# A two-layer relational graph network on one core: which engine copies turned rows, sums and row numbers, and how two queues share the copying of single rows

## The chip, the cores and the metric

The kernel runs on one core of one Trainium2 chip. The core has five engines that work side by side, each in the order of its own instructions: TensorE (PE in the profile; PEld are its weight loads), VectorE (DVE), ScalarE (ACT), GpSimd (POOL) and SyncE (SP). ACT, SP and POOL also issue DMAs, each on a queue of its own (ACTq, SPq, POOLq in the profile). The metric is the device time of one run in microseconds (us); for the kernel before, the median of three runs is 23771.16 us.

## The reference

Two relational graph layers over the same 800,000 edges and 50,000 nodes of 128 features, then a residual and a layer norm; cut to what matters:

```python
def _rgcn_layer(h, src, dst, rel, basis, w_comp, loop_w, bias):
    W = jnp.einsum('rb,bio->rio', w_comp, basis)          # 16 relations from 8 bases
    seg = dst.astype(jnp.int32) * N_REL + rel.astype(jnp.int32)
    agg = jax.ops.segment_sum(h[src], seg, num_segments=N_ENT * N_REL)
    agg = agg.reshape(N_ENT, N_REL, -1)
    msg = jnp.einsum('nri,rio->no', agg, W)
    return jax.nn.relu(msg + h @ loop_w + bias)

h = _rgcn_layer(x, src, dst, rel, basis1, w_comp1, loop_w1, bias1)
h = _rgcn_layer(h, src, dst, rel, basis2, w_comp2, loop_w2, bias2)
out = _layernorm(x + h)
```

The kernel is given 850,000 edges sorted by `dst`, among them one loop (src = dst) for each node. It takes the loops out and treats them apart as "own" rows.

## The kernel before

**Tiles, half chunks, chunks.** In each layer the 800,000 remaining edges are cut into 6250 tiles of 128 edges. Five tiles (`PER`) are a half chunk, ten a chunk; there are 1250 half chunks and 625 chunks (`C`). For each tile the 128 source rows, 512 bytes each, are brought from memory (from `x` in the first layer, from `H1`, named `H` in the profile, in the second) into a buffer `g`, and TensorE multiplies them with `hot`, a 128 x 96 matrix that VectorE has made from the edges' weights and targets (8 bases times a window of 12 nodes; line 1145). The products of a half chunk stand in one bank `pa` and are copied to `aT` (line 1101: by ACT in the first and last eight chunks, by DVE in between, `COPIED`). For four chunks at a time `aT` is multiplied with the bases (line 816), the sum is copied out (`by_slot`, line 821, ACT), turned (line 826), spread to nodes by DVE (`slots`, line 799) and added up per group of 512 nodes (`pn`, line 861). Beside this runs the work on own rows: a group's 512 rows are turned by TensorE (line 746), copied out (`hT`, line 752, ACT), multiplied with the bases (line 766), weighted and summed by DVE (lines 773 and 781).

**How rows come.** Most tiles are gathered by GpSimd: one indirect DMA per tile (line 187), whose 128 row numbers stand in a column of `at`. `at` holds numbers for 20 tiles and is made from the 16-bit list `src` by a cast on ACT (line 1075), three buffers in turn. The ring of `g` has 30 buffers, so a gather waits for the product that read its buffer 30 tiles before. The fifth tile of some half chunks is not gathered: `takers` gives every ninth half chunk to SP and, shifted by four, every ninth to ACT (`SPANS = (9, 9)`). `row_by_row` copies its 128 rows one at a time: a load of 32 row addresses from `far` into registers (line 1041), then 32 DMAs of 512 bytes, each with its address from a register (line 1048), four times. Each of the two queues has three buffers for this (`HELD`). In the program a copy is written in between the other work, a few rows after each product, over the nine half chunks before half chunk q - 8 (`LEAD`).

**Order.** All engines run under an order written out by hand: what the Python loop issues first stands first on its engine. So an ACT copy stands behind the row DMAs that were issued before it, and the row DMAs behind it wait while it waits.

**The beginning.** The edge list is turned into `src`, `far` and the other lists in pieces of rows (`ROWS`: half chunks 0 to 15, 16 to 119, and so on). In the first layer a step of `later_rows` is taken per chunk, and a piece is forced to be done at chunk c when 2 * (c + FETCH + earliest) goes beyond it, with `earliest` = 10.

Of the kernel before, what the change touches and what calls it, by code (L numbers as in the profile page):

```python
# [55 lines left out]
S = K * WN  # L56
# [4 lines left out]
LK = 64  # L61
LBITS = 10
FETCH = 2
WIDE = 20
AT = 8
PER = 5
Q = AT // 2
# [1 line left out]
WEIGHTS = AT * PER * 8  # L69
BITS_AT_ONCE = BANK - WEIGHTS  # L70
RING = 6
SPANS = (9, 9)
LEAD = 8
THEN = 3
COPIED = 8
# [6 lines left out]
BATCH = 4  # L82
# [11 lines left out]
def tile_rgcn_resnorm(  # L94
# [15 lines left out]
    nc = tc.nc  # L110
# [4 lines left out]
    C = -(-M // (K * P))  # L115
# [91 lines left out]
    src = consts.tile([P, 2 * C * HALF], U16, name="src")  # L207
# [4 lines left out]
    ]  # L212
    came = [[tc.alloc_semaphore(f"came{i}_{j}") for j in range(SEMS)] for i in range(len(APART))]
    uses = [0] * len(APART)
    earliest = (max(SPANS) + LEAD + 1) // 2 + 1
    far = consts.tile([P, len(ROWS), P], I32, name="far")

    def takers():

        of, first = {}, max(SPANS) + LEAD + 6  # L220
        for i, span in enumerate(SPANS):
            for q in range(first + span * i // len(SPANS), 2 * C - LEAD, span):
                while q in of:
                    q += 1
                of[q] = i
        return of

    taken_by = takers()
# [383 lines left out]
    def chunked():  # L612
        with (
# [5 lines left out]
            def ks(c):  # L619
                return min(K, -(-M // P) - c * K)  # L620

            ALONE, halves_of = C - BATCH - 1, [None]

            def nodes(g):
                return min(GN, N - g * GN) // J
# [21 lines left out]
            def told_apart(of, by, width, c, name):  # L647

                k = sum(ks(i) for i in range(c, min(c + Q, C)))
                apart = hp.tile([P, Q * K, width], U8, name=name, bufs=1)[:, :k]  # L650
                nc.vector.tensor_tensor(
                    apart,
                    of[:, None, :width].to_broadcast([P, k, width]),
                    by[:, c * K : c * K + k, None].to_broadcast([P, k, width]),
                    op=OP.is_equal,
                )
                return apart
# [70 lines left out]
            def from_itself(g, of, n):  # L728

                m = nodes(g)  # L730
                at, rows_in = g % T * (P // T), m // A
                if g == 0:
                    load_own(0, T, of)
                h = owns[at : at + rows_in]
                if g % T == 0:
                    for some in loop_weights(g, n):
                        if some is not None:
                            lws[:] = [some]
                        yield
                else:  # L740
                    yield
                lw = lws[0]
                po = ps_o.tile([P, BANK], F32, name="po")
                few = P // A
                for i in range(A * J):
                    nc.tensor.transpose(  # L746
                        po[:, i * few : i * few + rows_in], h[:, i, :], ident[at : at + rows_in, at : at + rows_in]
                    )
                    if i % (2 * A) == 2 * A - 1:
                        yield  # L750
                hT = sb.tile([P, J, P], F32, name="hT", bufs=2)
                nc.scalar.copy(  # L752
                    hT.rearrange("d j (p a) -> d a j p", a=A)[:, :, :, :rows_in],
                    po.rearrange("d (a j p) -> d a j p", a=A, j=J)[:, :, :, :rows_in],
                )
                hTs[g] = hT
                yield
                ls = sb.tile([P, J, D], F32, name="ls")
                lss[g] = ls
                few = BANK // D  # L760
                if g == 0:
                    nc.vector.tensor_copy(by[:, NB, :], BIAS[n])
                for j in range(J):
                    for b in range(0, NB, few):
                        hb = ps_o.tile([P, BANK], F32, name="po")
                        nc.tensor.matmul(  # L766
                            hb[:m],
                            hT[:, j, :m],
                            BASIS[n][:, b : b + few, :].rearrange("p b d -> p (b d)"),
                            start=True,  # L770
                            stop=True,
                        )
# [8 lines left out]
                    nc.vector.tensor_reduce(ls[:m, j, :], by[:m].rearrange("p b d -> p d b"), AX.X, OP.add)  # L781
                    yield
# [27 lines left out]
            def slots_of_batch(c, aT, st, n):  # L810

                for _ in range(2):
                    yield
                ps = ps_o.tile([P, BANK], F32, name="po")
                for b in range(NB):
                    nc.tensor.matmul(  # L816
                        ps[:, : BATCH * S], BASIS[n][:, b, :], aT[:, b, :], start=b == 0, stop=b == NB - 1
                    )
                yield
                by_slot = sb.tile([P, BATCH * S], F32, name="by_slot", bufs=1)  # L820
                nc.scalar.copy(by_slot, ps[:, : BATCH * S])
# [56 lines left out]
            def finish(g, n):  # L878

                m = nodes(g)  # L880
                ls = lss.pop(g)[:m]
                total = sums.pop(g)[:m].rearrange("p (j d) -> p j d", j=J)
                nc.vector.tensor_tensor(total if n else ls, total, ls, op=OP.add)
                if n == 0:
                    yield
                    nc.scalar.activation(ls, ls, AF.Relu)
                    for _ in range(THEN):
                        yield
                    nc.sync.dma_start(of_group(H1, g), ls)
                else:  # L890
                    nc.vector.scalar_tensor_tensor(ls, total, 0.0, xws.pop(g)[:m], op0=OP.max, op1=OP.add)
                    yield
                    yield from normed(ls, J, m, ls, sb)
                    for _ in range(THEN):
                        yield
                    nc.sync.dma_start(of_group(out, g), ls)  # L896
                yield

            def done(steps):
                for _ in steps:  # L900
# [39 lines left out]
            for n, of in enumerate((x, H1)):  # L940
# [82 lines left out]
                def row_by_row(i):  # L1023
# [1 line left out]
                    by, kind = APART[i]  # L1025
                    flat = bass.AP(tensor=of.tensor, offset=of.offset, ap=[[1, N * D]]).bitcast(U8)
                    mine = sorted(q for q in taken_by if taken_by[q] == i)
                    for q, before in zip(mine, [mine[0] - SPANS[i], *mine]):
                        while now[1] < before - LEAD:
                            yield  # L1030
                        steps = PER * (q - before)
# [23 lines left out]
                        held[q * PER + PER - 1] = to, sem, 16 * P * (use // SEMS + 1), group  # L1055
                        assert now[1] < q

                def place_in_ring(t):
# [10 lines left out]
                def numbers(b):  # L1069

                    m = min(WIDE, tiles - b * WIDE)
                    if m <= 0:
                        return
                    at = hp.tile([P, WIDE], I32, name="at", bufs=3)[:, :m]
                    made = nc.scalar.copy(at, src[:, b * WIDE : b * WIDE + m])  # L1075
# [21 lines left out]

                def taken_out():

                    by_vector = COPIED <= now[0] < C - COPIED  # L1100
                    (nc.vector.tensor_copy if by_vector else nc.scalar.copy)(*to_take)  # L1101

                numbered, held = {}, {}
                numbers(0)
                now, made = [0, 0], [0]
                owning = own_of_all()
                copying = [row_by_row(i) for i in range(len(APART))]
                for c in range(C):
                    now[0] = c
                    if n == 0 and c:  # L1110

                        next(coming, None)
                        while ready[0] + 1 < len(ROWS) and 2 * min(C, c + FETCH + earliest) > ROWS[ready[0] + 1]:
                            next(coming)
                    if c == 0:
                        fetch(range(RING * PER))
# [261 lines left out]
```

## Time and profile before

| | |
|---|---|
| median of 3 runs | 23771.16 us (23735.37 to 23829.01) |
| the profiled execution | 23546.47 us, of it 23544.3 us span |
| PE busy | 11586.5 us (49%) |
| DVE busy | 11688.0 us (50%) |
| ACT busy (copies and activations, without issuing DMAs) | 838.5 us (4%) |
| POOL busy | 11364.1 us (48%) |
| gathers by POOL | 5979 in each layer |
| rows copied one at a time by SP, by ACT | 17408 and 17280 in each layer |

Issuing DMAs is not counted as busy: how full the queues of SP and ACT are is seen in the timeline, where a row such as "SPq L1048 DMA_DIRECT2D g<-in_x_dram x64" is a stretch in which 64 single rows were issued (register loads between them are inside the stretch). In groups, "| a, b | c <-X d" reads: busy for a us in total, mean b ns of one, c us of idle time of the engine just before, of which X ended d.

### The profile page before, as it was taken

The page shows a single profiled execution, that of the slowest core. Times are in us where ns is not written, and L with a number is a line of the kernel's source. Part 1 is how long each engine was busy: PE and PEld are TensorE (multiplying, and loading weights), DVE is VectorE, ACT ScalarE, POOL GpSimd, SP SyncE. Part 2 cuts the span into 40 slices and gives each one's busy share as a digit, 9 for nine tenths or more (in the row PEclk, how much of TensorE's full clock was granted, in tenths as well). Part 3 has the DMA queues.
Part 4 walks back from the last instruction along what each step waited for, and adds up shares of the span by engine and source line. Part 5 has one row for each costly group of instructions (what it writes and reads, how often), then busy time and mean ns, then how long its engine had stood idle before and what let it go on. Part 6 is the DMA issues. An engine that isn't in the chain of part 4 may idle for free. (4 is left out here: it accounts for less than half of the span.)

```text
span 23544.3 us, 262043 instructions
## 1 busy us (share of the span) xinstructions
PE 11586.5 (49%) x43954; PEld 7419.2 (32%) x43954; DVE 11688.0 (50%) x14173; ACT 838.5 (4%) x1873; POOL 11364.1 (48%) x11991
## 2 busy tenths in 40 slices
PE   4544445444554544444554444444544444444445
PEld 3333333333333333233333333332332333333233
DVE  5555555555544444444544444444444444444445
ACT  0000000000000000000000000000000000000000
POOL 5544445444544444444454444444444444444444
PEclk7776677776677676676767776776766777766767
DMA  2111111111111111111111111111111111111111
GB/s 58 50 47 43 46 46 49 48 44 44 47 44 40 40 39 40 39 39 39 42 45 43 42 42 42 42 42 41 42 42 42 43 42 41 42 41 42 42 42 41
DMA packets 591750, 1014.42 MB, mean 43 GB/s; under 512 B 270531, under 2 KB 342979, under 8 KB 583794
## 3 DMA queue, kind: packets, MB, share of 16 engines
q0 software_dynamic: 384528, 791.33, 13.3%
q1 hardware_dynamic: 133308, 186.60, 2.5%
q10 hardware_dynamic: 72208, 19.62, 0.4%
q14 instruction: 1353, 11.08, 0.2%
q8 instruction: 353, 5.78, 0.1%
HBM read 924.87 MB, written 71.59 MB: 42 GB/s over the span
## 5 line engine op out<-in xcount | busy, mean ns | idle before, releaser
L187 POOL DMA_INDIRECT g<-H,at x5979 | 5658.7, 946 | 6136.5 <-PE pa L1145 3621.1
L187 POOL DMA_INDIRECT g<-in_x_dram,at x5979 | 5680.7, 950 | 5939.1 <-PE pa L1145 3438.7
L1145 PE MATMUL pa<-hot,g 128*128 128x96 f32 x25000 | 4289.6, 317 | 5679.3 <-DMA g<-H 2934.2
L1145 PEld LDWEIGHTS pa<-hot,g 128*128 128x128 f32 x25000 | 4239.8, 236 | 7638.2 <-DMA g<-H 3007.6
L773 DVE TENSOR_TENSOR by<-po,lw 128x512 f32<-128x512 f32 x1568 | 1074.7, 686 | 6412.4 <-PE po L766 4721.4
L861 PE MATMUL pn<-slots,own 120*128 120x512 f32 x4128 | 2738.5, 789 | 2075.2 <-issue 1117.4
L816 PE MATMUL po<-aT,basis 128*128 128x480 f32 x4960 | 2572.1, 681 | 1366.1 <-DVE aT L1101 752.6
L766 PE MATMUL po<-basis,hT 128*128 128x512 f32 x3136 | 2118.3, 764 | 1753.8 <-ACT hT L752 924.0
L1101 DVE COPY aT<-pa 128x480 f32<-128x480 f32 x2436 | 1567.6, 648 | 2672.5 <-PE pa L1145 2143.6
L816 PEld LDWEIGHTS po<-aT,basis 128*128 128x128 f32 x4960 | 1122.5, 233 | 2626.5 <-issue 2478.6
L781 DVE TENSOR_REDUCE ls<-by 128x128 f32<-128x1152 f32 (+1 forms) x784 | 1653.6, 2109 | 549.1 <-DMA out_dram<-ls 444.1
L668 DVE TENSOR_REDUCE fixed<-terms 128x80 f32<-128x1280 f32 x1250 | 1864.6, 1492 | 30.3
L639 DVE TENSOR_TENSOR terms<-kinds,fixed 128x1280 f32<-128x1280 uint8 x1250 | 1848.2, 1479 | 10.9
L861 PEld LDWEIGHTS pn<-slots,own 120*128 120x128 f32 x4128 | 884.8, 243 | 2749.4 <-issue 1753.9
L952 DVE TENSOR_TENSOR hot<-fixed,own 128x960 f32<-128x960 f32 x1250 | 1438.7, 1151 | 21.3 <-remote 3.0
L766 PEld LDWEIGHTS po<-basis,hT 128*128 128x128 f32 x3136 | 595.2, 236 | 1803.4 <-ACT hT L752 936.8
L799 DVE TENSOR_TENSOR slots<-po,which 120x1024 f32<-120x1024 f32 (+1 forms) x630 | 760.9, 1208 | 441.4 <-remote 304.8
L826 PE MATMUL po<-ident,by_slot 128*120 128x128 f32 x1240 | 311.5, 343 | 743.5 <-DVE by L773 423.0
L1075 ACT CAST at<-src 128x20 int32<-128x20 uint16 x626 | 129.5, 207 | 12082.0 <-issue 8490.2
L826 PEld LDWEIGHTS po<-ident,by_slot 128*120 128x120 f32 x1240 | 190.9, 188 | 764.1 <-issue 634.0
L840 DVE TENSOR_SCALAR own<-col,node 120x256 f32<-120x256 f32 (+1 forms) x1250 | 423.2, 339 | 8.6 <-PE pn L861 7.9
L746 PE MATMUL po<-ident,h_own 32*128 32x32 f32 x3136 | 328.2, 249 | 60.1 <-issue 54.1
(144 smaller groups left out, 3556.2 us busy)
## 6 DMA issues: line engine op xcount, KB each, us to landing
g<-in_x_dram SPq DMA_DIRECT2D x17408, 0.5 KB
g<-H SPq DMA_DIRECT2D x17408, 0.5 KB
g<-in_x_dram ACTq DMA_DIRECT2D x17280, 0.5 KB
g<-H ACTq DMA_DIRECT2D x17280, 0.5 KB
g<-in_x_dram,at POOLq DMA_INDIRECT x5979
g<-H,at POOLq DMA_INDIRECT x5979
H<-ls SPq DMA_DIRECT2D x97, 256.0 KB
xw<-in_x_dram SPq DMA_DIRECT2D x97, 256.0 KB
```

Of the source, the lines that this page charges most:

```text
L187: return nc.gpsimd.indirect_dma_start(out=to, out_offset=None, in_=of, in_offset=bass.IndirectOffsetOnAxis(ap=idx, axis=0))
L639: nc.vector.tensor_tensor(terms, kinds[:, :, None, :].to_broadcast([P, k, NB, NR]), table[:, None, :, :].to_broadcast([P, k, NB, NR]), op= ...
L668: nc.vector.tensor_reduce(to[:, : ks(i)], terms, AX.X, OP.add)
L766: nc.tensor.matmul(hb[:m], hT[:, j, :m], BASIS[n][:, b : b + few, :].rearrange("p b d -> p (b d)"), start=True, stop=True,)
L773: nc.vector.tensor_tensor(by[:m, b : b + few, :], hb[:m].rearrange("p (b d) -> p b d", d=D), lw[:m, j, g % T, b : b + few, None].to_broadc ...
L781: nc.vector.tensor_reduce(ls[:m, j, :], by[:m].rearrange("p b d -> p d b"), AX.X, OP.add)
L799: nc.vector.tensor_tensor(to[:k], of[:k, :, None, :].to_broadcast([k, pair, J, D]), which[:k, c : c + pair, :, None].to_broadcast([k, pair ...
L816: nc.tensor.matmul(ps[:, : BATCH * S], BASIS[n][:, b, :], aT[:, b, :], start=b == 0, stop=b == NB - 1)
L861: nc.tensor.matmul(sums[g], own, of[:k].rearrange("s j d -> s (j d)"), start=c == first(g), stop=c == final(g),)
L952: nc.vector.tensor_tensor(hot[:, : ks(c)], pm[:, : ks(c), :, None].to_broadcast([P, ks(c), NB, WN]), own[:, : ks(c), None, :].to_broadcast ...
L1101: (nc.vector.tensor_copy if by_vector else nc.scalar.copy)(*to_take)
L1145: product = nc.tensor.matmul(pa[:, i * NB * WN : (i + 1) * NB * WN], row, hot[:, k + i].rearrange("e b w -> e (b w)"), start=True, stop=Tr ...
```

## The change

VectorE makes three kinds of copies that ScalarE made: `hT`, `by_slot` and `at`, except in the first and last eight chunks of a layer. The spans become 9.25 half chunks for SP and 8.75 for ACT. And at the beginning the second piece of rows is forced in chunk 3, where it was forced in chunk 1 (`SOONEST` = 4 in the place of `earliest` = 10, which keeps its value). The assertions are not part of the program that runs.

```diff
+SOONEST = 4
-SPANS = (9, 9)
+SPANS = (9.25, 8.75)
...
-    earliest = (max(SPANS) + LEAD + 1) // 2 + 1
+    earliest = (round(max(SPANS)) + 1 + LEAD + 1) // 2 + 1
...
-        of, first = {}, max(SPANS) + LEAD + 6
+        of, first = {}, round(max(SPANS)) + LEAD + 6
         for i, span in enumerate(SPANS):
-            for q in range(first + span * i // len(SPANS), 2 * C - LEAD, span):
+            at = first + span * i / len(SPANS)
+            while at < 2 * C - LEAD:
+                q = int(at)
                 while q in of:
                     q += 1
                 of[q] = i
+                at += span
...
-                nc.scalar.copy(
+                copy_by()(
                     hT.rearrange("d j (p a) -> d a j p", a=A)[:, :, :, :rows_in],
...
-                nc.scalar.copy(by_slot, ps[:, : BATCH * S])
+                copy_by()(by_slot, ps[:, : BATCH * S])
...
+            def copy_by():
+
+                return nc.vector.tensor_copy if COPIED <= now[0] < C - COPIED else nc.scalar.copy
...
-                    for q, before in zip(mine, [mine[0] - SPANS[i], *mine]):
+                    for q, before in zip(mine, [mine[0] - round(SPANS[i]), *mine]):
...
-                    made = nc.scalar.copy(at, src[:, b * WIDE : b * WIDE + m])
+                    made = copy_by()(at, src[:, b * WIDE : b * WIDE + m])
...
-                        while ready[0] + 1 < len(ROWS) and 2 * min(C, c + FETCH + earliest) > ROWS[ready[0] + 1]:
+                        soon = FETCH + (earliest if ready[0] else SOONEST)
+                        while ready[0] + 1 < len(ROWS) and 2 * min(C, c + soon) > ROWS[ready[0] + 1]:
                             next(coming)
```

What moves on the engines. On ACT's queue in the first layer, around one Relu of a finished group (the same group in both); "1x512 x17" are 17 single rows in a row, `far` the load of 32 addresses. Before:

```order
L1048 DMA g_122<-in_x_dram 1x512 x9
L886 ACTIVATE ls<-ls 128x512
L1048 DMA g_122<-in_x_dram 1x512 x3
L1075 CAST at<-src 128x20
L1048 DMA g_122<-in_x_dram 1x512 x17
L821 COPY by_slot<-po 128x480
L1048 DMA g_122<-in_x_dram 1x512 x3
L1041 TENSOR_LOAD far
L1048 DMA g_122<-in_x_dram 1x512 x32
```

And of the change:

```order
L1057 DMA g_121<-in_x_dram 1x512 x2
L891 ACTIVATE ls<-ls 128x512
L1057 DMA g_121<-in_x_dram 1x512 x30
L1050 TENSOR_LOAD far
L1057 DMA g_121<-in_x_dram 1x512 x32
L1050 TENSOR_LOAD far
L1057 DMA g_122<-in_x_dram 1x512 x32
```

The casts and copies that stood between the rows are gone; between two Relus ACT now issues rows and nothing else. Over the whole program SP issues 33792 rows and 1056 loads (before 34816 and 1088), ACT 35584 and 1112 (before 34560 and 1080); POOL gathers 11958 tiles in both.

On DVE at the same group, of the change; `ls<-pn,ls` is the group's last sum, `aT` the copy of a half chunk's products, `by` and `ls` the work on own rows:

```order
L673 TENSOR_REDUCE fixed<-terms 128x80
L757 COPY hT<-po 128x4x128
L888 TENSOR_TENSOR ls<-pn,ls 128x512
L961 TENSOR_TENSOR hot<-fixed,own 128x960
L845 TENSOR_SCALAR own<-col_128,node_126 120x128
L1114 COPY aT<-pa 128x5x8x12
L1089 CAST at<-src 128x20
L778 TENSOR_TENSOR by<-po,lw 128x512
L1114 COPY aT<-pa 128x5x8x12
L643 TENSOR_TENSOR terms<-kinds,fixed 128x1280
```

Without `hT` and `at` this is the order of before. Of `at`, `by_slot` and `hT`, 610, 306 and 192 stand on DVE now, and 16, 4 and 4 on ACT (before 626, 310 and 196 on ACT).

At the beginning, on TensorE, before (`both` is the first product that makes the second piece of rows, g_95 the buffer of the tenth tile):

```order
L1145 MATMUL pa<-hot,g_94 128x96
L1145 MATMUL pa<-hot,g_95 128x96
L483 MATMUL pa<-ident,both 128x104 x5
L483 MATMUL pa<-ident,l_word 128x104 x5
L483 MATMUL pa<-ident,relf 128x104 x5
```

And of the change (g_115 is the buffer of the thirtieth tile, `h_own` are own rows):

```order
L1159 MATMUL pa<-hot,g_114 128x96
L1159 MATMUL pa<-hot,g_115 128x96
L751 MATMUL po<-ident,h_own 128x32 x8
L487 MATMUL pa<-ident,both 128x104 x5
L487 MATMUL pa<-ident,l_word 128x104 x5
L487 MATMUL pa<-ident,relf 128x104 x5
```

The second piece stood behind ten tiles and stands behind thirty. In SP's order the loads for the first own rows (`lrel`, `h_own`) now stand ahead of the loads of the second run of edges (`d_i` and three more), where they stood behind them; the first row copy stands behind all of these in both.

More of the change, by code (lines that the diff above doesn't have):

```diff
@@ L620, in ks @@
                 return min(K, -(-M // P) - c * K)
-            ALONE, halves_of = C - BATCH - 1, [None]
+            ALONE, halves_of, now = C - BATCH - 1, [None], [0, 0]
             def nodes(g):
@@ L649, in told_apart @@
                 k = sum(ks(i) for i in range(c, min(c + Q, C)))
+                assert ready[0] + 1 == len(ROWS) or 2 * min(c + Q, C) <= ROWS[ready[0] + 1]
                 apart = hp.tile([P, Q * K, width], U8, name=name, bufs=1)[:, :k]
@@ L1056, in row_by_row, with known @@
                         assert now[1] < q
+                def known(t):
+                    return ready[0] + 1 == len(ROWS) or t // PER < ROWS[ready[0] + 1]
                 def place_in_ring(t):
@@ L1073, in numbers @@
                         return
+                    assert n or known(b * WIDE + m - 1)
                     at = hp.tile([P, WIDE], I32, name="at", bufs=3)[:, :m]
-                    made = nc.scalar.copy(at, src[:, b * WIDE : b * WIDE + m])
+                    made = copy_by()(at, src[:, b * WIDE : b * WIDE + m])
                     for group in read_by.pop(len(numbered_all) - 3, ()):
@@ L1098, in taken_out @@
                 def taken_out():
-                    by_vector = COPIED <= now[0] < C - COPIED
-                    (nc.vector.tensor_copy if by_vector else nc.scalar.copy)(*to_take)
+                    copy_by()(*to_take)
                 numbered, held = {}, {}
                 numbers(0)
-                now, made = [0, 0], [0]
+                now[:], made = [0, 0], [0]
                 owning = own_of_all()
```

## The prediction

> **What bounds the kernel now.** I read first who waits for whom on TensorE, then the chain of work that ended last, then the timelines of the two copying queues. The two largest waits of TensorE, and what the row copies (line 1048) hold up in all:
>
> ```profile
> PE pa L1145 <- DMA g<-H: 2934.2, 121, 41.5
> PE pa L1145 <- DMA g<-in_x_dram: 2288.7, 94, 38.6
> L1048 SPq DMA_DIRECT2D g<-in_x_dram x17408: 1/228/1477, 103.9 to 11666.0; - x198
> L1048 ACTq DMA_DIRECT2D g<-in_x_dram x17280: 2/228/1450, 145.3 to 11532.5; - x199
>   PE pa L1145: 5280.2, 221
> ```
>
> TensorE stands 5.2 ms for rows that come one at a time, 221 waits of some 24 us. Whose rows? The chain, in the window from 19100 to 23400 us (the walk back gets no further than about 19 ms):
>
> ```profile
> by line: SPq L1048 50.1%; issue 35.2%; SPq L1041 7.6%; ACTq L1048 1.3%; PE po L816 0.9%; PE pa L1145 0.8%; DMA g<-H 0.7%; PE po L766 0.5%; PE pn L861 0.4%; SPq L896 0.3%; SPq L860 0.3%; SPq L723 0.3%; ACTq L1041 0.2%; DVE ls L781 0.2%; DVE
> ```
>
> Rows and address loads of SP are 58% of it, ACT's 1.5%; the "issue" pieces stand between SP's rows. Does SP ever wait itself? The longest of its own waits, and 200 us of its queue:
>
> ```profile
> SPq L295 <- DVE picked L422: 59.2, 1, 59.2
> SPq L889 <- ACT ls L886: 43.4, 1, 43.4
> ...
> 9000.41 31.15 SPq L1048 DMA_DIRECT2D g<-in_x_dram  x64
> 9031.57 0.69 SPq L889 DMA_DIRECT2D H<-ls  x1
> 9032.98 69.84 SPq L1048 DMA_DIRECT2D g<-in_x_dram  x91
> 9102.92 0.33 SPq L723 DMA_DIRECT2D h_own<-in_x_dram  x1
> 9103.35 67.41 SPq L1048 DMA_DIRECT2D g<-in_x_dram  x108
> 9170.79 0.34 SPq L889 DMA_DIRECT2D H<-ls  x1
> 9171.23 27.95 SPq L1048 DMA_DIRECT2D g<-in_x_dram  x44
> ```
>
> It issues without a pause. **SP's queue is the bound**; TensorE, VectorE and GpSimd, each half idle, run in its time. ACT's queue in the same stretch begins so (row pieces and what stands between them):
>
> ```profile
> 9001.11 19.25 ACTq L1048 DMA_DIRECT2D g<-in_x_dram  x38
> 9020.45 0.21 ACT L1075 CAST at<-src 128x20 int32<-128x20 uint16 x1 [39.12 <-issue]
> 9020.53 7.91 ACTq L1048 DMA_DIRECT2D g<-in_x_dram  x17
> 9028.48 1.07 ACT L752 COPY hT<-po 128x512 f32<-128x512 f32 x1 [7.82 <-PE po L746]
> 9036.71 0.56 ACT L821 COPY by_slot<-po 128x480 f32<-128x480 f32 x1 [7.16 <-PE po L816]
> 9036.78 24.30 ACTq L1048 DMA_DIRECT2D g<-in_x_dram  x37
> ```
>
> Between 9028.44 and 9036.78 ACT issues no row: `by_slot` waits for TensorE, and the rows behind it wait too. Over these three row pieces ACT spends 51.46 us on 92 rows, 0.56 us each; SP's four pieces above are 196.35 us for 307 rows, 0.64 us each.
>
> **What a row costs.** It depends on GpSimd. A stretch with gathers all through and one without (windows 8998 to 9006 and 9008 to 9027):
>
> ```profile
> 8998.00:9006.00 8.00, 0.00 (x0) 0.00 (x0) 0.00 (x0) 0.00 (x0) 4.72 (x5) 0.50 0.20 50
> 8998.98 5.63 SPq L1048 DMA_DIRECT2D g<-in_x_dram  x4
> 8999.69 5.62 ACTq L1048 DMA_DIRECT2D g<-in_x_dram  x4
> ...
> 9008.00:9027.00 19.00, 4.21 (x22) 3.80 (x22) 0.71 (x2) 0.21 (x1) 0.00 (x0) 0.50 0.01 3
> 9010.22 16.76 SPq L1048 DMA_DIRECT2D g<-in_x_dram  x44
> ```
>
> The fifth pair is POOL. While it gathers, both queues need 1.4 us a row; without it SP needs 0.381 us, its address load included. At that quiet price SP's 34816 rows are 13.26 ms; of the span of 23.54 ms the other 10.3 ms, 0.86 us for each of the 11958 gathers, are slowed stretches.
>
> **The change, part by part.** The sum is made against the profiled execution, 23546.47 us, which is 225 us under the median; I carry the same difference over to the median.
>
> *Spans.* SP loses 1024 rows and 32 loads (eight half chunks, four in each layer), ACT gets them. The gathers stay 11958, so I take the slowed stretches to stay as long as they are and price the rows as quiet ones: 1024 x 0.381 = **-390 us**. The other end is SP's mean, 23544.3 / 34816 = 0.676 us, hence -692 us. The quiet price is nearer, since the slowing comes with gathers.
>
> *ACT's queue gets denser.* It has 1024 rows more and no pauses at copies. Where gathers run the two queues move rows at one pace (4 in 5.63 us, 4 in 5.62 us), so I allow that a row of ACT there pushes one of SP into quiet time. Gathers cover 11958 x 1.25 us (one starts every 1.25 us below) = 14.9 ms, 63% of the span:
>
> ```profile
> 9000.60 0.95 POOL L187 DMA_INDIRECT g<-in_x_dram,at  x1 [0.30 <-issue]
> 9001.86 0.94 POOL L187 DMA_INDIRECT g<-in_x_dram,at  x1 [0.30 <-issue]
> ```
>
> That is at most 0.63 x 1024 x 0.381 = 246 us, at least nothing; ACT was issuing in most of that time already, so I take a quarter, **+60 us**.
>
> *Ends of the layers.* With the new spans SP's last copy of a layer is for half chunk 1234, before it was 1238 (23 + 9 x 135, and 23 + 9.25 x 131). Four half chunks more per layer pass with SP empty, at no less than five gathers each: 8 x 6.25 = **+50 us** (0 to 75, the latter at today's 9.4 us per half chunk).
>
> *Copies on DVE.* What moves, by ACT's rows, and the nearest DVE rows:
>
> ```profile
> L752 ACT COPY hT<-po 128x512 f32<-128x512 f32 x196 | 207.8, 1060 | 2924.9 <-issue 1955.1 <-PE po L746 429.1 <-remote 275.9
> L821 ACT COPY by_slot<-po 128x480 f32<-128x480 f32 x310 | 174.9, 564 | 3080.1 <-PE po L816 1294.5 <-issue 1037.1 <-PE pa L1145 486.9
> L1075 ACT CAST at<-src 128x20 int32<-128x20 uint16 x626 | 129.5, 207 | 12082.0 <-issue 8490.2 <-PE pa L1145 2359.0 <-remote 570.5
> L1101 DVE COPY aT<-pa 128x480 f32<-128x480 f32 x2436 | 1567.6, 648 | 2672.5 <-PE pa L1145 2143.6 <-remote 460.9 <-PE po L746 32.6
> L883 DVE TENSOR_TENSOR ls<-pn,ls 128x512 f32<-128x512 f32 x97 | 66.4, 685 | 229.5 <-remote 144.7 <-PE pa L1145 42.5 <-PE pn L861 26.5
> ```
>
> 192 x 0.685 + 306 x 0.648 + 610 x 0.207 = 456 us on DVE, 1.7 us in each of SP's 272 periods. It lies under TensorE's 24 us wait for SP's rows: **0**, and 456 us if that cover were gone. DVE now stops at `hT` and `by_slot` until TensorE has made them; queued behind are `hot`, `aT` and the own rows, for which TensorE waits. It stops at `aT` twice a chunk anyway. TensorE's own waits for a late `hT` (next row) only move to the next wait for SP's rows: no gain by themselves.
>
> ```profile
> PE po L766 <- ACT hT L752: 924.0, 66, 29.4
> ```
>
> The Trainium skill, "SBUF — State Buffer", section "Who interferes with whom", speaks against the cast: copies and casts of one SBUF operand on VectorE can take the port pair that GpSimd needs, and hold it for the instruction. No run here shows it; by that rule 610 casts, each holding up at most one gather of 0.95 us, would cost GpSimd 580 us, which its idle half takes in, and SP nothing.
>
> *Beginning.* Before, TensorE stood until the second piece of rows was made, and SP began its first copy after it:
>
> ```profile
> 95.44 1.10 PE L483 MATMUL pa<-ident,both 104*128 104x104 f32 x5 [49.51 <-DVE both L471]
> 97.77 0.29 DVE L494 TENSOR_SCALAR far<-both 104x128 int32<-104x128 f32 x1
> 103.93 26.02 SPq L1048 DMA_DIRECT2D g<-in_x_dram  x37
> ```
>
> Now twenty tiles' products come ahead of it, but so do, on DVE, the weights of two more chunks and of the first own rows, by the order of the change thirteen instructions, two each of 1.48, 1.49 and 1.15 us (lines 639, 668, 952) and seven smaller ones, about 14 us. `far` and SP's first row come that much later. As SP is the bound, this is a loss: **+14 us** (8 to 20). TensorE's head start is worth nothing, since it waits for SP's first copy anyway.
>
> Sum: -390 + 60 + 50 + 0 + 14 = **-266 us**: 23280 us in a profiled execution, **23505 us** in the median. With each term at its better and its worse end it is -374 to -49, that is 23397 to 23722.
>
> **The rivals.**
>
> 1. *The slowed stretches shrink with the rows* (a row costs SP its mean price). For it: of SP's 196.35 us above, 307 rows at the quiet price explain 117, and the rest, 40%, is slowing that its rows bore. Against: the gathers stay. -692 + 64 = -628: 23143 us.
>
> 2. *What slows the queues is common to them,* so that handing rows from one to the other changes nothing. For it: both had 4 rows in 5.6 us. Against: in the quiet stretch they issued at the same time at full speed. Displacement at its full 246 us leaves -390 + 246 + 64 = -80, 23691 us; with nothing saved it is +64, 23835 us. The Trainium skill says this more strongly, "DMA: Bandwidth & Descriptors", section "Issuing engines are not separate DMA queues": all DMAs run on the same 16 DMA engines, whichever engine starts them, and several issuers save issue time alone. By that rule the time stays; the trace agrees in gathers and not between them.
>
> 3. *Longer runs of gathers.* ACT's late `hT` and `at` break GpSimd's runs today. Without these breaks the runs between two SP waits get longer, and a long run is where a row costs 1.4 us. If the 0.86 us per gather grow by 2.6%, 0.022 us, the 266 us are gone: 23771 us.
>
> 4. *ACT becomes the bound; slower.* It has 35584 rows, and 664 us at its ends (to 145.3, from 11532.5 to 11852.9 and from 23346.5 us on; the second layer's row below). Up to (23280 - 664) / 35584 = 0.636 us a row it stays hidden. Its 0.56 us above come with pauses in which its queue rested; without pauses it may pay SP's 0.64 us, and 0.66 us, between this and SP's mean of 0.676, make 23485 + 664 = 24150 us profiled, 24375 us in the median. Against: it lies below SP's price today in the same stretch.
>
> ```profile
> L1048 ACTq DMA_DIRECT2D g<-H x17280: 2/228/1412, 11852.9 to 23346.5; - x199
> ```
>
> 5. That the change doesn't do what it says is excluded by the order of its instructions, but for the beginning, which is 14 us either way.
>
> **How the numbers follow.** Forecast 0.58, rival 1 0.12, rival 2 0.10, rival 3 0.10, rival 4 0.10. About 0.5%, 119 us, can be told from no change. Of the forecast's 0.58, 0.55 lies beyond it (below 23652 us), 0.03 within; rival 1 is faster; rival 2 gives 0.02 faster and 0.08 the same; rival 3 0.01 faster, 0.06 the same and 0.03 slower; rival 4 is slower. So faster 0.70, same 0.17, slower 0.13. The likeliest case's own range is 23397 to 23722. The range goes down to -692 (23079) and up to 23835, rival 2's worse end; rival 4 and a little below are left out, some 0.15.
>
> **What would show it.** The chain: still SP's rows and loads at over half of the late window. SP's queue without pauses, 264 copies in place of 272, with a longer time per copy (23280 / 264 = 88.2 us; now 23544 / 272 = 86.6). No `hT` among TensorE's longest waits. ACT's pauses between rows mostly gone and its last rows of a layer before SP's. DVE up by 350 to 560 us. It is wrong if TensorE's waits for rows are now ended by ACT's (rival 4), if the quiet price or the 0.86 us per gather has moved by more than 3% (rivals 1 to 3), or if DVE's stops at `by_slot` show up as waits of TensorE for `hot` or `aT`.

## The result: 0.9932 of the time before

The changed kernel takes 23611.39 us (median; 23604.99 to 23621.76), the kernel before beside it 23792.90 us: a ratio of 0.9932, with a 95% interval of 0.9920 to 0.9944, or 181 us less. The forecast was 23505 us, its own range 23397 to 23722.

The profiled execution of the changed kernel is 23609.02 us, *above* that of before (23546.47 us), though the medians say 181 us below. The two profiles must therefore not be subtracted from each other; why is shown in the second group of experiments. What can be read is where the kernel waits. The groups of waits of TensorE, which answer to the first two lines shown of before (line 1159 is now the product):

```profile
PE pa L1159 <- DMA g<-H: 2959.5, 118, 39.0
PE pa L1159 <- DMA g<-in_x_dram: 2834.1, 106, 45.9
...
PE po L821 <- DVE at L1089: 370.0, 31, 45.8
...
PE po L771 <- DVE hT L757: 194.6, 25, 43.7
```

TensorE's two waits for single rows are 5.8 ms in this profile, 5.2 in that of before. Its wait for `hT` is down from 924 us to 195 and is no longer among the ten longest. The chain of waits from 19100 to 23400 us, by line:

```profile
by line: SPq L1057 51.5%; issue 35.7%; SPq L1050 7.8%; PE pa L1159 0.7%; PE po L821 0.6%; PE po L771 0.5%; DMA g<-H 0.5%; SPq L901 0.5%; PE pn L866 0.4%; SPq L865 0.3%; SPq L728 0.2%; DVE ls L786 0.1%; SPq L685 0.1%; another core or an unkn
```

It is SP's queue still, at 59.3% with its loads (before 57.7%), and no row of ACT is in what the line shows. The single rows by queue and layer (count, shortest/median/longest ns, first and last start), and how long TensorE waited for them in all:

```profile
L1057 ACTq DMA_DIRECT2D g<-in_x_dram x17792: 1/228/1411, 154.9 to 11689.1; - x200
L1057 SPq DMA_DIRECT2D g<-in_x_dram x16896: 1/228/1478, 118.5 to 11761.6; - x199
L1057 SPq DMA_DIRECT2D g<-H x16896: 1/228/1473, 11868.5 to 23492.8; - x199
  PE pa L1159: 5820.5, 228
```

ACT's last row of the first layer starts 72.5 us before SP's; it was ahead in before too, by 133.5 us. And the three copies on VectorE (busy us, mean ns, idle time before):

```profile
L757 DVE COPY hT<-po 128x512 f32<-128x512 f32 x192 | 202.7, 1056 | 189.2 <-remote 150.4 <-issue 16.3 <-PE pa L1159 16.0
L826 DVE COPY by_slot<-po 128x480 f32<-128x480 f32 x306 | 198.8, 650 | 396.7 <-PE po L821 262.4 <-PE pa L1159 45.4 <-remote 35.5
L1089 DVE CAST at<-src 128x20 int32<-128x20 uint16 x610 | 119.0, 195 | 0.0
```

They cost VectorE 521 us by themselves; its busy time grew by 390 us in all. It stood 397 us ahead of `by_slot`, 189 us ahead of `hT` and not at all ahead of `at`.

### The profile page after: what moved, and what is told of

Same layout as the page of the kernel before. It is cut to its first block, busy times and chain, and to the rows that moved or that the text cites. A ratio compares the mean times of both kernels' runs of the same rounds, so it can differ in the third digit from the quotient of the medians.

```text
span 23607.1 us, 261491 instructions
## 1 busy us (share of the span) xinstructions
PE 11660.4 (49%) x43954; PEld 7412.4 (31%) x43954; DVE 12078.0 (51%) x15281; ACT 347.4 (1%) x765; POOL 11333.1 (48%) x11991
## 3 DMA queue, kind: packets, MB, share of 16 engines
q0 software_dynamic: 384528, 791.33, 12.8%
## 4 chain that ended last, share of the span: by engine, by line
SPq 36%; issue 22%; PE 2%; ACTq 1%; DVE 1%; DMA 0%; another core or an unknown queue 0%; POOL 0%; ACT 0%; DVEq 0%; POOLq 0%
SPq L1057 31%; SPq L1050 5%; ACTq L1057 1%; PE pa L1159 0%; PE po L821 0%; PE pn L866 0%; PE po L771 0%; DMA g<-H 0%; SPq L901 0%; SPq L728 0%; SPq L865 0%; DVE ls L786 0%; POOL g L188 0%; ACTq L1050 0%
## 5 line engine op out<-in xcount | busy, mean ns | idle before, releaser
L866 PE MATMUL pn<-slots,own 120*128 120x512 f32 x4128 | 2846.8, 817 | 2691.6 <-issue 1572.9
L961 DVE TENSOR_TENSOR hot<-fixed,own 128x960 f32<-128x960 f32 x1250 | 1437.4, 1150 | 14.6
L826 DVE COPY by_slot<-po 128x480 f32<-128x480 f32 x306 | 198.8, 650 | 396.7 <-PE po L821 262.4
L751 PEld LDWEIGHTS po<-ident,h_own 32*128 32x128 f32 x3136 | 297.7, 175 | 141.2 <-issue 123.4
L757 DVE COPY hT<-po 128x512 f32<-128x512 f32 x192 | 202.7, 1056 | 189.2 <-remote 150.4
```

The source lines that it names most:

```text
L866: nc.tensor.matmul(sums[g], own, of[:k].rearrange("s j d -> s (j d)"), start=c == first(g), stop=c == final(g),)
L961: nc.vector.tensor_tensor(hot[:, : ks(c)], pm[:, : ks(c), :, None].to_broadcast([P, ks(c), NB, WN]), own[:, : ks(c), None, :].to_broadcast ...
```

## Experiments, first group: each part alone, and the bound

The theory was the prediction's: SP's queue bounds, the spans give the gain, the copies and the beginning are nearly free. These four ran on one chip, the kernel before beside them at 23509.6 us.

**e1_spans: the spans alone.** Against the changed kernel:

```diff
-SOONEST = 4
+SOONEST = 10
-                copy_by()(
+                nc.scalar.copy(
                     hT.rearrange("d j (p a) -> d a j p", a=A)[:, :, :, :rows_in],
...
-                copy_by()(by_slot, ps[:, : BATCH * S])
+                nc.scalar.copy(by_slot, ps[:, : BATCH * S])
...
-                    made = copy_by()(at, src[:, b * WIDE : b * WIDE + m])
+                    made = nc.scalar.copy(at, src[:, b * WIDE : b * WIDE + m])
```

> The kernel before with the spans 9.25 and 8.75 alone; ScalarE keeps all its copies. Theory (SP's queue is the bound): SP has 1024 rows less, so most of the change's 181 us is here, 150 to 340 us faster than before, and TensorE still waits for SP's rows. Rival (the spans pay only with the copies gone from ACT, which is else late): no more than 60 us faster, and TensorE's waits for rows ended by ACT's in a third of the cases or more.

Measured 22961.71 us, ratio 0.9767 (0.9754 to 0.9781): -548 us. That is far beyond what was expected, and three times what the whole change brought on the chip where it was measured. How long TensorE waited for rows in this kernel, from the view of the row copies:

```profile
  PE pa L1159: 4310.5, 198
```

And from its list of waits, TensorE's for `hT` and GpSimd's for ACT's `at`:

```profile
PE po L771 <- ACT hT L757: 1230.7, 71, 34.8
POOL g L188 <- ACT at L1089: 651.0, 108, 15.8
```

TensorE waits 1.0 ms less for rows than before, and 0.3 ms more for `hT` (before 924 us).

**e2_copies: the copies alone.**

```diff
-SOONEST = 4
+SOONEST = 10
-SPANS = (9.25, 8.75)
+SPANS = (9, 9)
```

(with the old rounding of the half chunks, so that the same ones are copied as before)

> The kernel before with the three kinds of copies on VectorE alone; spans 9 and 9. Theory: SP's queue is untouched, so nothing is gained: from 0 to 100 us slower (ACT's denser queue pushes SP's rows). Rival (late copies on ACT cost time by themselves, 924 us of TensorE's waits): 100 us or more faster.

Measured 23675.97 us, ratio 1.0073 (1.0061 to 1.0086): 166 us slower, more than the upper end. TensorE's wait for rows in the same view is 0.8 ms longer than before (5280.2 us; that profile is of the same kind of chip, as the second group shows):

```profile
  PE pa L1159: 6049.4, 240
```

So one part of the change is a gain and another a loss. On this chip the two make -382 us by themselves; the whole change made -181 us on another chip, and it was not run on this one.

**e3_soon: the beginning alone.** Against the changed kernel, `SOONEST = 4` staying:

```diff
-SPANS = (9.25, 8.75)
+SPANS = (9, 9)
...
-                copy_by()(by_slot, ps[:, : BATCH * S])
+                nc.scalar.copy(by_slot, ps[:, : BATCH * S])
```

(`hT` and `at` likewise, and the old rounding of the half chunks)

> The kernel before with the second piece of rows forced in chunk 3 alone. Theory: SP's first row copy comes about 14 us later, 5 to 25 us slower, so no difference that can be told. Rival (TensorE's stall of 49.5 us at the beginning is saved): 30 to 50 us faster.

Measured 23502.75 us, ratio 1.0000 (0.9991 to 1.0008). SP's first row starts where it does in the changed kernel, 14.6 us later than before (from the timeline of SP):

```profile
118.55 41.46 SPq L1057 DMA_DIRECT2D g<-in_x_dram  x56
```

An interval of some 20 us to both sides cannot tell 14 us from nothing; it excludes that the beginning alone costs a large part of what lies between the spans and the whole change.

**e4_half: half the single rows.** In the changed kernel:

```diff
-SPANS = (9.25, 8.75)
+SPANS = (18.5, 17.5)
```

> The changed kernel with spans 18.5 and 17.5: half as many half chunks have a tile copied by rows, SP 16896 rows, ACT 17664, GpSimd 12230 gathers in place of 11958. Theory (SP's queue is the bound): SP needs 16896 x 0.381 us + 12230 x 0.86 us = 17.0 ms and is no bound any more; TensorE's 5.8 ms of waits for rows go, and the time falls to between 18 and 21 ms, where gathers, TensorE and VectorE set it. Rival (the gathers are the bound behind the row copies: a gather in place of a row copy costs the time that the copies were there to save): no faster than 23.6 ms, GpSimd without pauses.

Measured 18434.94 us, ratio 0.7841 (0.7830 to 0.7853): 5.1 ms less, with 272 gathers more. SP's rows of the first layer:

```profile
L1057 SPq DMA_DIRECT2D g<-in_x_dram x8448: 1/228/1468, 117.5 to 9122.6; - x197
```

And the longest waits of TensorE:

```profile
PE pn L866 <- issue: 1919.3, 518, 15.4
PE po L821 <- DVE aT L1114: 835.2, 118, 16.1
PE pn L866 <- DVE slots L804: 834.8, 130, 15.6
```

No wait for a single row is among them. That the single rows set the time of the changed kernel is thereby shown. That it is SP's queue of the two, e1 shows: there ACT was handed 1024 of SP's rows and the kernel got 2.3% faster. This version beats both by far; what bounds it was not followed.

## Experiments, second group: what is dear in the copies

Three theories. **A**: ACT's late `at` broke GpSimd's runs of gathers, and rows late in a long run are dear (rival 3). **B**: ACT's stops at `hT` and `by_slot` helped (as it was put down, because its queue rests there). **C**: VectorE's own stops there make `hot` and `aT` late. All four kernels ran on a second chip, with the kernel before at 23801.65 us.

**e5_after: the changed kernel again**, without an edit.

> The changed kernel again, unaltered, as the measure for the three that follow on the same chip. Measured once at 0.993 of the kernel before; the spans alone gave 0.977 on another chip. All theories expect 0.991 to 0.996 here (some -170 us). If it comes out below 0.985, most of what the copies seemed to cost in combination was a difference between chips.

Measured 0.9933 (0.9921 to 0.9946), as in the result. Each ratio is to the kernel before on its own chip. The spans alone were not run on this chip, nor the changed kernel on the first, so the distance of 0.0166 to e1's 0.9767, some 390 us, can be in part a difference between the chips. What this chip shows by itself follows.

**e6_at and e7_products: the new spans with one kind on VectorE.** Against the changed kernel, both with `SOONEST = 10`; e6, and behind it e7:

```diff
-                copy_by()(
+                nc.scalar.copy(
                     hT.rearrange("d j (p a) -> d a j p", a=A)[:, :, :, :rows_in],
...
-                copy_by()(by_slot, ps[:, : BATCH * S])
+                nc.scalar.copy(by_slot, ps[:, : BATCH * S])
```

```diff
-                    made = copy_by()(at, src[:, b * WIDE : b * WIDE + m])
+                    made = nc.scalar.copy(at, src[:, b * WIDE : b * WIDE + m])
```

> The new spans with one of the three kinds of copies on VectorE: `at`, the row numbers; `hT` and `by_slot` stay on ScalarE. Theory A (ScalarE's late `at` broke GpSimd's runs of gathers, and rows late in a long run are the dear ones): the cost comes with `at`; 0.988 to 0.996, GpSimd's waits for ScalarE gone (650 us with the spans alone). Theory B (ScalarE's stops at `hT` and `by_slot` rested its queue, and SyncE's rows went faster meanwhile) and theory C (VectorE itself stops at `hT` and `by_slot`, and `hot` and `aT` behind them are late): `at` is free; 0.974 to 0.981, as with the spans alone.

> The new spans with `hT` and `by_slot` on VectorE, and `at` on ScalarE. Theory A: nearly free, 0.974 to 0.982, if GpSimd still waits for ScalarE's `at` (by more than 300 us); if those waits go too, because ScalarE is no longer held up ahead of `at`, theory A expects the cost here as well. Theories B and C: the cost is here; 0.988 to 0.996.

Measured 0.9835 (0.9822 to 0.9848) and 0.9912 (0.9899 to 0.9926). Against e5's 0.9933 on the same chip, moving `hT` and `by_slot` to VectorE beside `at` costs 0.0098, some 230 us; moving `at` beside them costs 0.0021, barely beyond the intervals. The main cost lies with `hT` and `by_slot`. A has at most a part, not the main one. In e7 GpSimd waits for ACT's `at` longer than in any other of these kernels, and the kernel is hardly faster than e5 for it:

```profile
POOL g L188 <- ACT at L1089: 2151.4, 212, 23.4
```

The prediction named a rule of the Trainium skill, "SBUF — State Buffer", section "Who interferes with whom", by which the casts on VectorE could hold GpSimd's port. Within e6 the 504 gathers that a cast overlaps take 952 ns in the mean, the others 946. As a group the gathers did not get longer; the groups of the gathers of `x` in e6 and, with the cast on ACT, in e1:

```profile
L188 POOL DMA_INDIRECT g<-in_x_dram,at x5979 | 5665.9, 948 | 5963.2 <-PE pa L1159 3532.8 <-issue 1623.8 <-remote 604.3
```

```profile
L188 POOL DMA_INDIRECT g<-in_x_dram,at x5979 | 5678.8, 950 | 5716.7 <-PE pa L1159 3141.5 <-issue 1643.6 <-remote 526.6
```

**e8_stops: VectorE copies, and ACT stops where it stopped before.** In the changed kernel:

```diff
+            def stop_of_act(of):
+
+                if COPIED <= now[0] < C - COPIED:
+                    nc.scalar.copy(sb.tile([P, 1], F32, name="stop", bufs=1), of[:, :1])
...
                 hTs[g] = hT
+                stop_of_act(po)
...
                 copy_by()(by_slot, ps[:, : BATCH * S])
+                stop_of_act(ps)
```

> The changed kernel, and at each `hT` and `by_slot` that VectorE copies ScalarE copies one column of the same product into a spare tile, so that its queue stops where it stopped before, while VectorE makes all three copies. Theory B: most of the cost is won back, 0.976 to 0.985. Theory A: GpSimd's runs stay as long as in the changed kernel, 0.990 to 0.997. Theory C: VectorE's stops stay, 0.990 to 0.998.

Measured 0.9844 (0.9829 to 0.9858): 498 useless copies of one column on ACT make the changed kernel 0.9% *faster*, back to where e6 is. C falls as the main cause, since VectorE's stops are all still there. TensorE's wait for rows (the product is line 1166 here):

```profile
  PE pa L1166: 4610.9, 209
```

And TensorE's waits for the stops:

```profile
PE po L772 <- ACT stop L909: 920.1, 73, 27.9
PE po L833 <- ACT stop L909: 401.0, 24, 30.1
```

The 1.2 ms that TensorE waits less for rows (e5: 5801.9 us) it now stands before the product that follows a stop. In all kernels with the new spans the ratio rises, within its intervals, with TensorE's wait for rows: 4.31 ms and 0.9767 (e1, on the first chip), 4.61 and 0.9844 (e8), 4.68 and 0.9835 (e6), 5.69 and 0.9912 (e7), 5.80 and 0.9933 (e5).

How can a wait of an engine off the path be worth time? I put each single row of SP in the traces to the gather under way when it starts (a gather's place lasts to the next one's start, that of the last in a run to 1.5 us after its end; a run has gaps of at most 0.6 us; all from SP's first single row to its last). Time with gathers, SP's rows in it, what was left for the time without gathers, and SP's rows per us by the gather's place in its run:

| kernel (chip) | with gathers | rows in it | rows left, in | 1st to 3rd | 4th to 6th | 7th on |
|---|---|---|---|---|---|---|
| before (first) | 16.44 ms | 18311 | 16504, 6.92 ms | 1.90 | 1.08 | 0.57 |
| e1, spans (first) | 16.49 ms | 18765 | 15026, 6.25 ms | 1.89 | 1.11 | 0.57 |
| e5, change (second) | 16.37 ms | 17057 | 16734, 7.10 ms | 1.81 | 1.01 | 0.51 |
| e8, stops (second) | 16.43 ms | 17658 | 16133, 6.78 ms | 1.84 | 1.02 | 0.51 |

The time with gathers is the same in all of them; the rows left cost 0.42 us each. Within a chip the time thus follows from one number, how many rows SP gets through while GpSimd gathers: the stops get 601 more through (252 us at 0.42 us; the profiled executions differ by 263), the spans alone 454 more than before. A row costs some 0.5 us at the beginning of a run; from the seventh gather on it costs 1.75 us on the first chip and 2 us on the second. The changed kernel has 4609 gathers from the seventh place on, e8 4378; more of its gathers fall on cheap places.

The places are half of the account. With e5's rows per gather in each of the three columns, e8's places alone would get some 300 rows more through, not 601; the others are more rows per gather at the same place, and why, no run shows. Nor do the places explain the loss of e2: it has 4594 gathers from the seventh place on, before 4595, and still 147 of SP's rows fewer get through.

One such run, from the timeline of e5, ten gathers long (the first and the last shown), with the rows of the two queues beside it:

```profile
9182.78 13.96 SPq L1057 DMA_DIRECT2D g<-in_x_dram  x16
9182.87 13.16 ACTq L1057 DMA_DIRECT2D g<-in_x_dram  x19
9182.98 0.94 POOL L188 DMA_INDIRECT g<-in_x_dram,at  x1 [25.33 <-PE pa L1159]
...
9194.23 0.94 POOL L188 DMA_INDIRECT g<-in_x_dram,at  x1 [0.30 <-issue]
```

The run began when TensorE's products gave buffers back; 0.87 us a row, against 0.42 without gathers.

The table also says why the two profiled executions don't compare: from the seventh place on, SP issues 0.57 to 0.58 rows per us in before, e1, e2 and e3, and 0.50 to 0.52 in e5 to e8. The profile of the changed kernel has 0.51, that of before 0.57: by this mark the first was taken on a chip like the second, the other on a chip like the first. The time of the latter, 23546 us, also lies beside the runs of before on the first chip (23451 to 23545) and not with those on the second (23764 to 23855).

## Experiments, third group: on a chip of another kind

Two theories were left for the stops. **R**: SP's rows go faster while ACT's queue rests. **P**: TensorE, held up by ACT, gives buffers back in smaller portions, and the gathers fall on cheaper places. The four kernels that follow ran on a third chip, on which **the kernel before takes 15759.72 us** (median of 16 runs, 15750.63 to 15768.23).

**e9_stops_free**: as e8, with the stops behind the finished copy.

```diff
-                stop_of_act(po)
+                stop_of_act(hT[:, 0])
...
-                stop_of_act(ps)
+                stop_of_act(by_slot)
```

> As the kernel with ScalarE's stops, but ScalarE's one-column copy reads the finished `hT` or `by_slot` in the place of TensorE's product, so that ScalarE's queue still stops there, while TensorE is no longer held up by ScalarE. Theory R (rest: SyncE's rows go faster because ScalarE's queue stops): the gain of the stops stays, 0.980 to 0.987. Theory P (pace: what helped was that ScalarE, late at its stop, held TensorE up; TensorE then stands less for row copies, frees fewer buffers at one blow, and more gathers fall on the first three places of a run, where a row is cheap): the gain is lost, 0.989 to 0.996, and TensorE's waits for row copies are back at 5.5 ms or more (4.6 with the stops, 5.8 without).

Measured 1.0000 (0.9991 to 1.0009) of the kernel before, which answers the question not at all, since the ground of both theories is missing here. SP's rows of the first layer and TensorE's wait for rows:

```profile
L1064 SPq DMA_DIRECT2D g<-in_x_dram x16896: 224/228/1351, 101.8 to 7790.3; - x199
  PE pa L1166: 376.2, 48
```

And of the timeline 25 us in which GpSimd gathered every 1.25 us (the first two of its gathers shown):

```profile
9020.66 25.43 SPq L1064 DMA_DIRECT2D g<-H  x63
9021.31 0.94 POOL L188 DMA_INDIRECT g<-H,at  x1 [0.30 <-issue]
9022.55 0.94 POOL L188 DMA_INDIRECT g<-H,at  x1 [0.30 <-issue]
```

SP issues a row every 0.40 us *through* the gathers. Nothing slows, and the waits of 5 ms are 0.4 ms.

R and P remain to be told apart by the traces of the second chip. Taking as rest every gap over 3.5 us between ACT's rows or address loads, ACT rests 1496 us in e8 and 1616 us in e5: the stops helped and gave its queue no more rest. In e2 it rests 2597 us, longer than in before (2258 us), and the kernel is slower. Nor do ACT's rows push SP's out while gathers run: e8 starts 20977 of ACT's rows there and e5 20293, so both queues gain together, and in e2 both lose (ACT 20176, before 20817). That speaks against R. P has the places for it, which are half of the gain; no run shows it alone, and what e2 loses neither explains.

**e10_half_act, e11_quarter, e12_few: fewer rows.**

```diff
-SPANS = (9.25, 8.75)
+SPANS = (18.5, 17.5)
```

e10, with the three kinds of copies on ACT as in e1; in e11 the changed kernel with (37, 35), in e12 with (300, 300), where each copy is spread over the 9 half chunks ahead of its own and no more.

> Spans of 18.5 and 17.5 with all three kinds of copies on ScalarE. Measured before with the copies on VectorE: 0.784 of the kernel before. Theory P: where SyncE's rows no longer bound the time, a late `hT` only delays TensorE, so the copies on ScalarE lose here: 0.790 to 0.815. If the copies on VectorE are dear for themselves (VectorE's time, or GpSimd's ports), this is faster: 0.765 to 0.780.

> The changed kernel with spans of 37 and 35: a quarter of its single rows, some 12365 gathers. If what the rows delay is still the price in the half (18.43 ms, GpSimd gathering in 81% of it), this is 16.5 to 18.2 ms. If the rows of the half already cost nothing, it is 18.3 to 18.8 ms, GpSimd's 135 gathers more being 0.17 ms.

> The changed kernel with five copies of 128 single rows by each queue in a layer, nearly every tile gathered by GpSimd (some 12480 gathers). At 1.25 us a gather these alone are 15.6 ms; with the waits for TensorE that the half still shows 17.0 to 19.0 ms. If single rows earn their place at all in the half, this is slower than the half and the quarter; above 20 ms if gathers one behind another cost more than 1.25 us each.

Measured 15398.72 us (0.9772, 0.9759 to 0.9785), 15573.52 us (0.9882, 0.9867 to 0.9897) and 15703.82 us (0.9965, 0.9952 to 0.9978). The expectations were for the other kind of chip; what can be read here is the bound. GpSimd's gathers in e10 and in e12, of the second layer:

```profile
L188 POOL DMA_INDIRECT g<-H,at x6115 | 5772.4, 944 | 1879.0 <-issue 1801.5 <-PE pa L1159 47.0 <-PE po L771 12.5
```

```profile
L188 POOL DMA_INDIRECT g<-H,at x6241 | 5891.1, 944 | 1914.6 <-issue 1813.1 <-PE pa L1159 52.1 <-PE po L771 10.1
```

In each it gathers without a break, one every 1.25 us: 12230, 12366 and 12482 gathers are 15.29, 15.46 and 15.60 ms, and the rest of each is 0.10 to 0.12 ms. There GpSimd is the bound, and from one of these three to the next each row copy that keeps a tile from it saves 1.1 to 1.3 us. Fewer gathers still do not help: the 11958 of the kernel before are 14.95 ms, and it takes 15.76. The half with the copies on VectorE was not run on this chip, so what the copies do there stays open. Half the rows is the best of the kernels run on either kind of chip: 0.784 (first, copies on VectorE) and 0.977 (third, copies on ACT).

## Why the forecast was right, and where it wasn't

**The total was right by luck, by two errors of opposite sign.** Forecast -266 us, measured -181, inside the own range; the terms were not. The parts as measured alone (-548, +166 and nothing) don't add up to -181 either; whether the copies cost more with the new spans or the chips differ, no run shows. The range itself has a slip: with ACT's density and the ends at nothing and the beginning at 8 us its better end is -382, 23389 us, in place of -374; nothing hangs on it.

- *The bound* (SP's queue): right, by e4 and e1. Right as well: no `hT` among TensorE's longest waits, VectorE up by 390 us (350 to 560 said), a copy by SP longer than before (23611 / 264 = 89.4 us, before 23793 / 272 = 87.5). ACT's last rows of a layer come before SP's, but they did in before too, so this shows nothing. One of its signs of being wrong did come: reckoned as in the prediction, the price per gather is 0.90 us in the changed kernel's profile, over 3% above 0.86. That profile is of the other kind of chip; on the first chip it is 0.84 in e1 and 0.87 in e2.
- *The spans* (-390, with +60 and +50 for ACT's density and the ends: -280): too small, -548 measured alone. A row taken from SP saved 0.535 us, between the quiet price and the mean. The quiet price itself was near (0.42 us, loads included); what failed is the step "I take the slowed stretches to stay as long as they are and price the rows as quiet ones". They stay as long (16.4 ms), but 454 more of SP's rows went through in them. *ACT's denser queue* (+60) was to push SP's rows out of the gathers; no run shows that, since in e1 more of SP's rows went through and in e2 ACT's own rows fell along with SP's.
- *The ends* (+50): right. SP pauses between the layers for 106.9 us and ends 114.3 us before the span; before it was 79.0 and 83.2 us, from the row below: together 59 us more.

```profile
L1048 SPq DMA_DIRECT2D g<-H x17408: 1/228/1450, 11745.0 to 23461.1; - x198
```

- *The copies on VectorE* (0): the step that failed. The 456 us on VectorE (521 measured) are hidden, as said, and e8 against e6 shows that its stops cost nothing that can be seen. Wrong was the sentence on TensorE's waits for a late `hT`, "only move to the next wait for SP's rows: no gain by themselves". They did move there, and it was not free: the copies cost 166 us alone, on the first chip, and with the new spans `hT` and `by_slot` cost some 230 us, on the second. What was missing in the step is how many rows SP gets through beside gathers, which the moved copies lower; half of this is accounted for by the places in e8, the rest stays open.
- *The beginning* (+14): right in the trace (SP's first row at 103.9 and 118.5 us), in the time not to be told.
- *Rivals.* For the spans, rival 1's terms (-692 and the ends' 50: -642) were nearer to the measured -548 than the forecast's -280, but its mechanism isn't there: the slowed stretches did not shrink, more rows went through them. Rival 2 falls: 1024 rows handed to the other queue gave 2.3%. The prediction put a rule of the Trainium skill, "DMA: Bandwidth & Descriptors", section "Issuing engines are not separate DMA queues", beside it and read it as "the time stays". That section of the Trainium skill says that several issuers save the time of issuing, and that this is usually small; here the issuing queue is the bound, and it isn't small. Rival 3 had the right sign, and rows late in a run are the dear ones; of the copies it names `hT` (with `by_slot`) is the larger part and `at` the smaller, and in e2 the copies cost time though no more gathers came late. Rival 4 falls: in e1 ACT has the same rows and the kernel is faster, and in the changed kernel the late chain is SP's.

## What to carry to other kernels

Price a moved copy not only by its time on the engine that takes it over: ask whom it used to hold up. Here 498 one-column copies that made an engine with slack wait gained 0.9%, so taking such a wait away can cost more than the copy. Split a change with several parts before keeping it, since here one part alone was worth three times the whole (on another chip); and run the two kernels on the same chip before subtracting their profiles.

## What the runs showed of the hardware

The same program, the kernel before, takes 23509.6, 23801.65 and 15759.72 us on three chips, lowest to highest within 0.4% on each. On the third, GpSimd's gathers don't slow the single rows of the other queues; on the first two a row costs 1.75 and 2 us late in a run of gathers, though gathers start every 1.25 us on all three. The gathers' transfers don't take longer either. The DMA queue of the gathers (packets, MB, share of 16 engines' span) in the changed kernel and in e9:

```profile
q0 software_dynamic: 384528, 791.33, 12.8%
```

```profile
q0 software_dynamic: 384528, 791.33, 22.7%
```

12.8% of 16 x 23607 us is 0.126 us a packet, 22.7% of 16 x 15758 us is 0.149 us: the packets take no longer where the rows are slow, and as a mean of the 16 the engines are mostly idle. The granted TensorE clock is 0.70 in before on the first two chips and 0.81 on the third, but in e4, on the first, it was 0.76, and rows late in a run cost 2.1 us. What differs between the chips, no run shows. A tuning of SP's and ACT's shares is thus a tuning to one kind of chip.
